# Two late turns of a local-attention loop put in the steady order, and the pool maxima of a later layer partly moved ahead and rebuffered

## The chip, the cores and the metric

The kernel runs on one core of one Trainium2 chip. The metric is device time of one launch in microseconds (us). The kernel before took 5015.74 us, the median of three runs (5015.45, 5015.74 and 5020.18). Five engines work beside each other: PE (TensorE, matrix products), DVE (VectorE), ACT (ScalarE), POOL (GpSimd) and SP (SyncE, which issues all DMA transfers, in one queue).

## The reference

The input is two images of 512 channels and 64 x 64 pixels, float32. Four residual layers follow one another, each `x = x + f(groupnorm(x))` with 32 groups:

- Layer 0, local and pooled attention with 8 heads of 64. Each pixel attends to its 3 x 3 neighbours and to 256 pooled tokens, with one softmax over both. A learned table adds to the nine local weights. The result goes through `W_proj`.
- Layer 1, deformable attention: offsets computed from the queries say where 256 keys are sampled from the image; then ordinary attention and an output product with `w_out`.
- Layer 2, a mixture of max pools. Seven pools with windows 1, 3, 5, 7, 9, 11 and 13 are made per channel, and a score of the channel mixes two neighbouring ones:

```
pools = jnp.stack([_maxpool_same(x, k) for k in KERNELS], axis=2)
...
return frac_b * b_out + frac_s * s_out + x
```

- Layer 3, linear attention with random exponential features (Favor), 256 features per head.

## The kernel before

Pixels are 4096 columns and channels are 4 chunks (KC) of 128 partitions. X holds the image and Y is a work area of the same size. A block is 512 columns (TB), one PSUM bank, and there are 8 blocks (NB). The two images are computed one after the other; `whole_net` calls layer0 to layer3 (L2748 to L2755) for each. All products are float32. A slower path (class General, up to L933) is compiled in behind a condition on the data and is not run here; what runs is class Net (from L934) with its helpers Queries and Local.

A tile framework schedules the program: by default it orders each engine's instructions by its own priorities. Inside `manual_schedule(engines={...})` the named engines run in the order in which the code issues. Buffers come from pools with a fixed number of copies, and a write waits until the last reader of the copy is done.

**Layer 0, class Local.** The work is cut into 16 units (4 chunks of channels by 4 strips of 1024 columns). `Local.run` (the loop at L2058) goes over turns i from -4 to 16. A turn interleaves stages of several units, one step of each in a round (`in_turn`, L51): norms and projections of unit i+3 (PE's L134), tap products of unit i+1 on DVE (`tap_products`, L2489: q times the shifted keys, into two product buffers `prods`), tap sums of unit i+1 on PE (`tap_sums`, L2527: into the one bank of the pool `l0t`; then DVE's L2536 multiplies, and ACT's L2538 takes the exponential out of that bank), softmax and values of unit i (`attend`, whose softmax sums are L2581 and L2584 and whose reciprocal chain on DVE is L2609 to L2612; L2616 and L2617 follow), and the weighting by the nine taps of unit i-1 (`weigh`, ACT L2656, DVE L2664, POOL L2669, which reads rows that SP fetches with L2640 and stores to a DRAM buffer `yd` with L2675).

`self.steady` (L2060) is true for turns 1 to 11. A steady turn runs PE in the written order, pairs the nine tap products as five DVE instructions of up to 1024 x 2 elements, spreads the steps of tap sums and projections over the rounds as a table says, and keeps the sums of two probabilities in two buffers of `sq`. Other turns run in the scheduler's order with nine single tap products. Turn 16 is in PE's written order as well. Unit 16 does not exist: turn 13 has no projections of queries and keys but the values of both of the last units, and turn 14 has the tap sums of the last unit. From turn 13 on `fetch_output` (L2231) loads W_proj into the four `sq` buffers, and turns 14, 15 and 16 begin the output products of the layer (`output`, L2242, L2258), which read `yd` back through SP (L2252).

**Layer 1.** After the attention blocks, `add_output` (L1215 on PE, L1218 and L1220 on DVE) writes the image back and takes its statistics. In the same loop DVE makes the first pool (window 3) for layer 2 in Y, by `maxima_across` and `maxima_down` (L1136 to L1152), through rows lent from the weights' buffer wkv. L1497 is the reciprocal of the softmax sums, which PE's L1505 spreads. The chain of small operations L1175 to L1207 (`pool_mixture`) works out the mixing weights, the last of which PE needs before layer 2 starts.

**Layer 2.** `pool_chunk` (L1363) runs per channel chunk. Steps j = 0 to 6 add the image and the six pools into eight PSUM banks, each as a product with a diagonal matrix: 8 blocks times two instructions of L1382 (ACT makes the diagonal, L1387). Each new pool from j = 2 is made on DVE from the last by a maximum of columns (`spread_max(h, last, 2)`) and one of rows; each is one operation of 128 x 3968 elements (L698), and ACT copies the two edges (L699). The pools pass through two buffers, and from chunk 1 on Y's last chunk is a third. From chunk 1, `maxima_below` (L1161 to L1166) first completes the rows of the first pool. Then ACT takes the sum out of the banks and, for chunks 0 to 2, its mean and variance come from sums (six small DVE operations per chunk, L1428 to L1436). In chunk 3 the eighth block's products of the first steps are held back, so that its bank serves for layer 3's group statistics (`stats_in_steps`: PE L965 and L970, DVE L966 to L972, POOL L973). Then DVE scales the first three parts of layer 3's two weight matrices by these (L978).

**Layer 3** begins with products of these scaled weights. SP loads its matrices Wk3 and Wv3 (L1359) and proj (L1521); L1522 is the first operation on proj.

Of the kernel before, what the change touches and what calls it, by code (L numbers as in the profile page):

```python
# [9 lines left out]
F32 = mybir.dt.float32  # L10
# [6 lines left out]
P = 128  # L17
# [916 lines left out]
class Net(General):  # L934
# [102 lines left out]
    def layer1(self, X, Y, d):  # L1037

        tc, nc, vec = self.tc, self.nc, self.vec
        with tc.tile_pool(name="l1", bufs=1) as sp:  # L1040
            wkv = sp.tile([P, KC, 2 * C], F32, name="wkv1")
# [4 lines left out]
            with tc.tile_pool(name="l1a", bufs=1) as wp, \  # L1046
# [6 lines left out]
            self.ahead = ExitStack()  # L1053
            dp = self.ahead.enter_context(tc.tile_pool(name="diags", bufs=1, side="right"))
            self.diags = cycle([dp.tile([P, P], F32, name=f"diag{i}") for i in range(2)])
            with tc.tile_pool(name="l1c", bufs=1) as late:

# [16 lines left out]
                with tc.tile_pool(name="l1b", bufs=2) as wp, \  # L1074
                        tc.tile_pool(name="l1s", bufs=6, space=PSUM) as pp, \
                        tc.tile_pool(name="l1o", bufs=2, space=PSUM) as ppo:
                    st = wp.tile([P, KC, NB, 6], F32, name="gn_st1", bufs=1)
                    w1 = wp.tile([P, KC, 32], F32, name="w1", bufs=1)
                    nc.sync.dma_start(w1, d["w1"].rearrange("(kc p) e -> p kc e", p=P))
                    w2 = wp.tile([32, C], F32, name="w2", bufs=1)  # L1080
                    nc.sync.dma_start(w2, d["w2"])
                    wo = wp.tile([P, KC, C], F32, name="wo1", bufs=1)
                    nc.sync.dma_start(wo, d["w_out1"].rearrange("(kc p) o -> p kc o", p=P))
                    steps = [(blk, cc) for blk in range(NB) for cc in range(KC)]
                    part = lambda blk, cc=slice(0, KC): Y[:, cc, blk * TB:(blk + 1) * TB]
                    flat = lambda a: a.rearrange("p k o -> p (k o)")
                    probs, totals, later = {}, {}, []
                    rows3 = flat(wkv)[:, :KC * 10 * W].rearrange("p (k y x) -> p k y x", k=KC, x=W)
                    ring = cycle([a[:, n:n + TB] for a, lo, hi in (
                        (flat(wq), 0, KC), (flat(wkv), 5, 8), (flat(feats), 0, 2),  # L1090
                        (wp.tile([P, 3 * TB], F32, name="totals", bufs=1), 0, 3))
                        for n in range(lo * TB, hi * TB, TB)]).__next__
                    for i in range(len(steps) + 4 + KC):
                        if i < len(steps):
                            blk, cc = steps[i]
                            probs[i], totals[i] = self.exponentials(part(blk, cc), keys[:, cc, :],
                                                                    ring, wp, pp)
                        if 1 <= i <= len(steps):
                            blk, cc = steps[i - 1]
                            self.attended(part(blk, cc), probs.pop(i - 1),  # L1100
                                          vals[:, :, cc * P:(cc + 1) * P], ppo)
                        at = lambda n: i >= n and (i - n) % KC == KC - 1 and (i - n) // KC
                        if (blk := at(1)) is not False and blk < NB:
                            r = self.inverse_sums([totals.pop(KC * blk + n) for n in range(KC)], wp,
                                                  pp)
                        if (blk := at(2)) is not False and blk < NB:
                            self.divided(part(blk), r, pp)
                        if (blk := at(3)) is not False and blk < NB:
                            later += [(blk, oc) for oc in range(KC)]
                        if later:  # L1110
                            blk, oc = later.pop(0)
                            self.add_output(X, wo, part(blk), blk, oc, st, pp)
                            if blk == NB - 1:
                                nc.vector.bn_aggr(self.mv[:, oc, :],
                                                  st[:, oc].rearrange("p b s -> p (b s)"))
                                if oc < 2:
                                    self.maxima_across(X, NB - 2, rows3, slice(oc, oc + 1))
                                    self.maxima_down(Y, NB - 2, rows3, slice(oc, oc + 1))
                            elif oc == KC - 1 and blk < NB - 2:
                                self.maxima_across(X, blk, rows3, slice(0, KC))  # L1120
                                self.maxima_down(Y, blk, rows3, slice(0, KC))
                    mixture = self.pool_mixture(w1, w2, wp, pp)
                    next(mixture)
                    self.maxima_across(X, NB - 1, rows3, slice(0, 1))
                    self.maxima_down(Y, NB - 1, rows3, slice(0, 1))
                    next(mixture)

    def maxima_across(self, X, blk, h, ks):
# [13 lines left out]
    def maxima_down(self, Y, blk, h, ks):  # L1142
# [7 lines left out]
        nc.vector.tensor_tensor(to, to, h[:, :, lo:rows + 1], ALU.max)  # L1150
        if blk == NB - 1:
            nc.vector.tensor_tensor(out[:, :, W - 1], h[:, :, rows], h[:, :, rows + 1], ALU.max)  # L1152

    def maxima_below(self, x, to, h, blk):

# [189 lines left out]

    def layer2(self, X, Y, d):

        self.w3 = self.ahead.enter_context(self.tc.tile_pool(name="l3w", bufs=2))
        self.wkv3 = [self.load3(d, name) for name in ("Wk3", "Wv3")]
        with self.tc.tile_pool(name="l2", bufs=1) as sp, \  # L1350
                self.tc.tile_pool(name="l2a", bufs=8, space=PSUM) as ppa:
            self.junk = sp.tile([P, TB], F32, name="pool_sq")
            self.accs = [ppa.tile([P, TB], F32, name=f"acc{b}", bufs=1) for b in range(NB)]
            for cc in range(KC):
                self.pool_chunk(X, Y, cc, self.mix[:, 7], self.mix[:, 8], self.mix[:, :7], sp)

    def load3(self, d, name):
        w = self.w3.tile([P, KC, C], F32, name="w3")
# [3 lines left out]
    def pool_chunk(self, X, Y, cc, c0, d0, wts, sp):  # L1362
# [2 lines left out]
        nc = self.nc  # L1365
        x2 = X[:, cc, :]
        image = lambda a: a.rearrange("p (y x) -> p y x", x=W)
        if cc == 0:
            self.scratch = sp.tile([P, N], F32, name="pool_h")
            self.pools = [sp.tile([P, N], F32, name=f"pool{i}") for i in range(2)]  # L1370
        else:
# [13 lines left out]
        def add(w, src, j):  # L1385
            dg = next(self.diags)
            nc.scalar.activation(dg, self.ident, AF.Copy, scale=w)  # L1387
            for b in range(NB):
# [3 lines left out]
                    product(b, dg, src, j)  # L1392
                while kept and j == 5 and b == 3:
                    product(*kept.pop(0))
            if len(kept) in (3, 5):
                next(stats, None)
            if len(kept) == 5:
                for w in self.wkv3:
                    self.scale_part(w, slice(0, KC - 1))

        add(c0[:, cc:cc + 1], x2, 0)
        flat = Y[:, cc, :]
        for j in range(1, 7):
            if j > 1:
                last, flat = image(flat), self.pools.pop(0)
                self.pools.append(flat)
                self.spread_max(h, last, 2)
                self.spread_max(image(flat), h, 1)
            add(wts[:, j, cc:cc + 1], flat, j)
        mv = self.mv[:, cc]  # L1410
        if cc == KC - 1:
# [8 lines left out]
        sums = sp.tile([P, 2, NB], F32, name="pool_sums", bufs=2)  # L1420
        shift = sp.tile([P, 1], F32, name="pool_shift", bufs=2)
# [10 lines left out]
        mean, var = mv[:, 0:1], mv[:, 1:2]  # L1432
        nc.vector.tensor_copy(mean, total[:, 0:1])
        nc.vector.tensor_tensor(shift, shift, mean, ALU.add)
        nc.vector.tensor_tensor(shift, shift, shift, ALU.mult)
        nc.vector.tensor_tensor(var, total[:, 1:2], shift, ALU.subtract)  # L1436

    def product_bound(self, q, keys, sp, pp):

# [528 lines left out]
class Local:  # L1968
# [78 lines left out]
    def run(self):  # L2047
# [311 lines left out]
    def projections(self, u, uvs, streams):  # L2359
# [506 lines left out]
```

## Time and profile before

The profile is one execution: it took 5015.88 us, of which the span from the first to the last instruction is 5014.0 us. PE's mean granted clock was 0.984 of full speed.

| what | value |
|---|---|
| median of three runs | 5015.74 us |
| the profiled execution | 5015.88 us |
| its span | 5014.0 us |
| DVE, ACT, POOL busy | 3074.1, 1816.8, 1859.1 us |
| a steady turn of layer 0 | 41.49 us |
| turns 12 and 13 of layer 0, image 1 | 45.90 and 50.32 us |
| layer 2, image 1 | 1486.9 to 1694 us |
| one operation L698 (128 x 3968) | 4.29 us |
| eight blocks of L1382 | 6.87 us |

The layers of image 1 lie at 31 to about 990 us (layer 0), to about 1487 (layer 1), to 1694 (layer 2) and to 2520 (layer 3); image 2 repeats them some 2489 us later. In the profile's rows an instruction is named by its line and its output and input tiles, and `xN` counts instructions in a group; a bracket at the end gives the idle time of the engine just before it and what ended that. A float32 product of one block is two PE instructions.

### The profile page before, as it was taken

What the parts mean: (1) busy time and instruction counts of PE and PEld (TensorE: products, weight loads), DVE (VectorE), ACT (ScalarE), POOL (GpSimd) and SP (SyncE); (2) the same over time, 40 slices, a digit from 0 to 9 for tenths busy, and PEclk for the clock granted to TensorE, in tenths of its full rate; (3) what the DMA queues carried; (4) which work ended last, traced back from release to release, by engine and by line L of the source; (5) the groups of instructions that cost most, each with busy time, mean ns of one, the idle gap of its engine ahead of it and who ended that gap; (6) DMA issues with size and microseconds to landing.
All of it is one profiled execution on the core that took longest, in us unless ns stands there. A gap on an engine that the chain in (4) does not pass through costs nothing. (4 is left out here: it accounts for less than half of the span.)

```text
span 5014.0 us, 48290 instructions
## 1 busy us (share of the span) xinstructions
PE 4771.4 (95%) x16883; PEld 1971.8 (39%) x16883; DVE 3074.1 (61%) x3958; ACT 1816.8 (36%) x3477; POOL 1859.1 (37%) x1220
## 2 busy tenths in 40 slices
PE   7999998999999999999999999989999999999998
PEld 3433332554334444433343333335543344444333
DVE  4367776744679533477732777767446794335776
ACT  1256664244323233322112566642443242333221
POOL 0046665501320145554500466654014101554554
PEclk9999999999999999999999999999999999999999
DMA  3035555500000000211120455555000000000111
GB/s 154 1 103 155 155 156 164 160 19 10 1 17 0 1 1 1 72 55 44 58 74 2 126 154 157 151 159 150 12 10 1 17 1 1 1 1 24 43 45 43
DMA packets 129440, 313.29 MB, mean 62 GB/s; under 512 B 23394, under 2 KB 36194, under 8 KB 127652
## 3 DMA queue, kind: packets, MB, share of 16 engines
q1 hardware_dynamic: 129188, 310.12, 21.6%
q8 instruction: 135, 2.21, 0.2%
q14 instruction: 117, 0.96, 0.1%
HBM read 260.73 MB, written 49.31 MB: 62 GB/s over the span
## 5 line engine op out<-in xcount | busy, mean ns | idle before, releaser
L134 PE MATMUL mm<-big,w 128*128 128x512 f32 x2496 | 1164.9, 610 | 16.3 <-DVE big L2448 11.5
L134 PEld LDWEIGHTS mm<-big,w 128*128 128x128 f32 x2496 | 452.6, 191 | 698.3 <-issue 557.2
L2669 POOL TENSOR_TENSOR late<-late,big 128x1024 f32<-128x1024 f32 x194 | 458.5, 2363 | 223.4 <-DVE big L2664 185.4
L2489 DVE TENSOR_TENSOR prods<-qs,big 128x1024 f32<-128x1024 f32 (+1 forms) x200 | 332.2, 1686 | 60.1 <-PE tap L2527 49.1
L1669 POOL TENSOR_TENSOR big<-big 128x512 f32<-128x512 f32 x224 | 277.8, 1273 | 219.4 <-ACT big L1660 219.4
L2664 DVE TENSOR_TENSOR big<-big,mm 128x512 f32<-128x512 f32 x388 | 253.1, 681 | 114.9 <-ACT mm L2656 107.0
L1660 ACT ACTIVATE big<-mm,ed 128x256 f32<-128x256 f32 x512 | 193.5, 489 | 233.1 <-DVE top L1656 200.7
L2656 ACT COPY mm<-big 128x512 f32<-128x512 f32 x432 | 245.8, 597 | 60.4 <-DMA big<-rows 25.1
L2574 POOL TENSOR_TENSOR late<-late 128x512 f32<-128x512 f32 x84 | 105.3, 1275 | 410.5 <-ACT late L2559 393.9
L2669 POOL TENSOR_TENSOR late<-late,tap 128x1024 f32<-128x1024 f32 x94 | 222.1, 2363 | 94.5 <-DVE tap L2664 80.1
L1472 POOL TENSOR_TENSOR wq<-prob 128x512 f32<-128x512 f32 x48 | 71.6, 1515 | 487.9 <-ACT prob L1469 476.5
L1656 DVE TENSOR_REDUCE top<-mm 128x1 f32<-128x512 f32 x256 | 159.0, 684 | 148.1 <-PE mm L1587 148.1
L1924 PE MATMUL mm<-k,w 128*128 128x512 f32 x512 | 235.1, 602 | 12.4 <-DVE k L1917 7.5
L134 PE MATMUL mm<-big,wq 128*128 128x512 f32 x512 | 236.7, 608 | 2.7 <-ACT off_t L1243 2.7
L1215 PE MATMUL mm<-big,wo 128*128 128x512 f32 x512 | 238.1, 611 | 0.0
L1382 PE MATMUL acc<-big,diag 128*128 128x512 f32 x512 | 228.7, 604 | 9.8 <-ACT diag L1387 4.6
L1634 PE MATMUL mm<-w,big 128*128 128x512 f32 x512 | 234.5, 601 | 0.0
L973 POOL TENSOR_TENSOR group_stats<-group_stats,cst 128x1 f32<-128x1 f32 (+1 forms) x20 | 20.2, 1025 | 566.4 <-DVE group_stats L972 510.2
L2527 PE MATMUL tap<-prods,cst 128*32 128x512 f32 x1152 | 189.6, 620 | 29.2 <-ACT late L2538 26.5
L1914 DVE RECIPROCAL psD<-psD 128x512 f32<-128x512 f32 x64 | 215.1, 3362 | 1.9
L134 PE MATMUL mm<-big,big 128*128 128x512 f32 x464 | 201.7, 594 | 0.5 <-DVE b_sr L1011 0.5
L1469 ACT ACTIVATE prob<-mm 128x512 f32<-128x512 f32 x256 | 133.2, 603 | 171.4 <-PE mm L1466 171.1
(428 smaller groups left out, 8114.1 us busy)
## 6 DMA issues: line engine op xcount, KB each, us to landing
big<-rows SPq DMA_DIRECT2D x432, 256.0 KB
tap<-rows SPq DMA_DIRECT2D x208, 256.0 KB
yd<-late SPq DMA_DIRECT2D x32, 512.0 KB
lost_all<-lost SPq DMA_DIRECT2D x128, 128.0 KB
out<-big SPq DMA_DIRECT2D x64, 256.0 KB
big<-in_W_kv SPq DMA_DIRECT2D x8, 1024.0 KB
rows<-late SPq DMA_DIRECT2D x64, 128.0 KB
big<-in_x SPq DMA_DIRECT2D x32, 256.0 KB
```

The lines of the kernel that those rows point to most:

```text
L134: self.nc.tensor.matmul(ps, w[:, kc, :], X[:, kc, blk * TB:(blk + 1) * TB], start=(kc == 0), stop=(kc == KC - 1))
L1215: nc.tensor.matmul(ps, w[:, kc, oc * P:(oc + 1) * P], att[:, kc, :], start=(kc == 0), stop=(kc == KC - 1))
L1382: nc.tensor.matmul(accs[b], dg, src[:, b * TB:(b + 1) * TB], start=(j == 0), stop=(j == 6))
L1634: nc.tensor.matmul(ps, X[:, kc, lo:lo + P], wv[:, kc, :], start=(kc == 0), stop=(kc == KC - 1))
L1660: nc.scalar.activation(f[:, t, :], pS[h][i][:, t % 2, :], AF.Exp, bias=ed[:, t, 2 * cc + h:2 * cc + h + 1])
L1669: nc.gpsimd.tensor_tensor(a, a, part, ALU.add)
L1914: nc.vector.reciprocal(psD, psD)
L1924: nc.tensor.matmul(ps, self.wo[:, kc, oc * P:(oc + 1) * P], qs[:, kc, :], start=(kc == 0), stop=(kc == KC - 1))
L2489: self.nc.vector.tensor_tensor(self.pair(u, k)[:, :n].rearrange("p k (y x) -> p k y x", x=W), bcast(qs.rearrange("p (y x) -> p y x", x=W), ...
L2656: nc.scalar.copy(ps, part)
L2664: nc.vector.tensor_tensor(part.rearrange("p (y x) -> p y x", x=W), self.vx[:, y:y + self.UY // 2, dx:dx + W], ps.rearrange("p (y x) -> p y ...
L2669: nc.gpsimd.tensor_tensor(out, out, t, ALU.add)
```

## The change

In layer 0, turns 12 and 13 count as steady (`units - 2` for `units - 4`), so they take PE's written order and all that hangs on `self.steady`. The table of the steps at which values are made gets two more entries, for the four values of turn 13.

```diff
-            self.steady = 1 <= i < units - 4
+            self.steady = 1 <= i < units - 2
...
-        made, taken = ((4, 6, 7, 8), (0, 2)) if self.steady else ((6, 7, 8, 9), (0, 3, 6, 9))
+        made, taken = ((4, 6, 7, 8), (0, 2, 4, 6)) if self.steady else ((6, 7, 8, 9), (0, 3, 6, 9))
```

In layer 1, the buffer wkv moves to a pool that lives until the end of layer 2 and serves there as the buffer h of column maxima (`self.scratch`). The first column maximum of chunk 0 (j = 2) is made in six pieces within layer 1's tail, and no longer in layer 2:

```diff
+        self.ahead, self.pooling = ExitStack(), ExitStack()
+        kept = self.pooling.enter_context(tc.tile_pool(name="kv1", bufs=1, side="right"))
+        wkv = kept.tile([P, KC, 2 * C], F32, name="wkv1")
+        self.scratch = wkv.rearrange("p k o -> p (k o)")
...
+                                for rows in ([(20, 32), (32, 44)], [(10, 20), (44, 55)],
+                                             [], [])[oc]:
+                                    self.across_rows(Y, slice(*rows))
...
                     self.maxima_down(Y, NB - 1, rows3, slice(0, 1))
+                    for rows in (0, 10), (55, W):
+                        self.across_rows(Y, slice(*rows))
                     next(mixture)
...
+    def across_rows(self, Y, rows):
+
+        image = lambda a: a.rearrange("p (y x) -> p y x", x=W)[:, rows]
+        self.spread_max(image(self.scratch), image(Y[:, 0, :]), 2)
```

In layer 2, chunk 0 has a third pool buffer, which is given up after it. Only then is the pool for layer 3's weights opened and Wk3 and Wv3 loaded. DVE runs chunk 3 in the written order. The statistics' steps stand in that order, the moments of chunks 0 to 2 are made at once in chunk 3, and ACT scales the weights in six copies:

```diff
+            with tc.tile_pool(name="l2f", bufs=1) as fp:
+                self.pools.append(fp.tile([P, N], F32, name="pool2"))
+                self.pool_chunk(X, Y, 0, c0, d0, wts, sp)
+                self.pools.pop(0)
+            self.w3 = self.ahead.enter_context(tc.tile_pool(name="l3w", bufs=2))
+            self.wkv3 = [self.load3(d, name) for name in ("Wk3", "Wv3")]
+            for cc in range(1, KC):
+                with (tc.manual_schedule(engines={mybir.EngineType.DVE}) if cc == KC - 1
+                      else nullcontext()):
+                    self.pool_chunk(X, Y, cc, c0, d0, wts, sp)
...
-            if len(kept) in (3, 5):
-                next(stats, None)
-            if len(kept) == 5:
-                for w in self.wkv3:
-                    self.scale_part(w, slice(0, KC - 1))
...
-                self.spread_max(h, last, 2)
+                if cc or j > 2:
+                    self.spread_max(h, last, 2)
                 self.spread_max(image(flat), h, 1)
+                if cc == KC - 1 and j in (4, 5):
+                    next(stats, None)
+                if cc == KC - 1 and j == 3:
+                    self.moments(sp)
+                if cc == KC - 1 and j == 5:
+                    for w in self.wkv3:
+                        for kc in range(KC - 1):
+                            nc.scalar.activation(w[:, kc], w[:, kc], AF.Copy,
+                                                 scale=self.stats[:, 1, kc:kc + 1])
...
-        total = sp.tile([P, 2], F32, name="pool_total", bufs=2)
-        nc.vector.tensor_reduce(total, sums, AX.X, ALU.add)
+
+    def moments(self, sp):
+
+        nc = self.nc
+        total = sp.tile([P, KC - 1, 2], F32, name="pool_total")
+        nc.vector.tensor_reduce(total, self.sums, AX.X, ALU.add)
```

The other five operations of `moments` are those of before, on three chunks' columns at once. The instructions' order on every engine outside these places is that of before.

More of the change, by code (lines that the diff above doesn't have):

```diff
@@ L1039, in layer1 @@
         tc, nc, vec = self.tc, self.nc, self.vec
+        self.ahead, self.pooling = ExitStack(), ExitStack()
+        kept = self.pooling.enter_context(tc.tile_pool(name="kv1", bufs=1, side="right"))
+        wkv = kept.tile([P, KC, 2 * C], F32, name="wkv1")
+        self.scratch = wkv.rearrange("p k o -> p (k o)")
         with tc.tile_pool(name="l1", bufs=1) as sp:
-            wkv = sp.tile([P, KC, 2 * C], F32, name="wkv1")
             nc.sync.dma_start(wkv, d["w_kv1"].rearrange("(kc p) o -> p kc o", p=P))
@@ L1052, in layer1 @@
                 self.query_and_sample(X, Y, wq, bq, grid, feats, top, wp, pp, ppk)
-            self.ahead = ExitStack()
-            dp = self.ahead.enter_context(tc.tile_pool(name="diags", bufs=1, side="right"))
+            dp = self.pooling.enter_context(tc.tile_pool(name="diags", bufs=1, side="right"))
             self.diags = cycle([dp.tile([P, P], F32, name=f"diag{i}") for i in range(2)])
@@ L1087, in layer1 @@
                     probs, totals, later = {}, {}, []
-                    rows3 = flat(wkv)[:, :KC * 10 * W].rearrange("p (k y x) -> p k y x", k=KC, x=W)
+                    rows3 = self.scratch[:, :KC * 10 * W].rearrange("p (k y x) -> p k y x", k=KC, x=W)
                     ring = cycle([a[:, n:n + TB] for a, lo, hi in (
@@ L1346, in layer2 @@
     def layer2(self, X, Y, d):
[L1348 to L1351, printed above, removed]
+        tc = self.tc
+        with tc.tile_pool(name="l2", bufs=1, side="right") as sp, \
+                tc.tile_pool(name="l2a", bufs=8, space=PSUM) as ppa:
             self.junk = sp.tile([P, TB], F32, name="pool_sq")
             self.accs = [ppa.tile([P, TB], F32, name=f"acc{b}", bufs=1) for b in range(NB)]
-            for cc in range(KC):
-                self.pool_chunk(X, Y, cc, self.mix[:, 7], self.mix[:, 8], self.mix[:, :7], sp)
+            self.sums = sp.tile([P, KC - 1, 2, NB], F32, name="pool_sums")
+            self.shifts = sp.tile([P, KC - 1], F32, name="pool_shift")
+            self.pools = [sp.tile([P, N], F32, name=f"pool{i}") for i in range(2)]
+            c0, d0, wts = self.mix[:, 7], self.mix[:, 8], self.mix[:, :7]
+            with tc.tile_pool(name="l2f", bufs=1) as fp:
[8 more added lines that the diff above has]
+                    self.pool_chunk(X, Y, cc, c0, d0, wts, sp)
+        self.pooling.close()
     def load3(self, d, name):
@@ L1367, in pool_chunk @@
         image = lambda a: a.rearrange("p (y x) -> p y x", x=W)
[L1368 to L1371, printed above, removed]
+        if cc:
             self.maxima_below(x2, Y[:, cc, :], self.scratch, NB - 1 if cc == 1 else NB - 2)
@@ L1419, in pool_chunk @@
             return
-        sums = sp.tile([P, 2, NB], F32, name="pool_sums", bufs=2)
-        shift = sp.tile([P, 1], F32, name="pool_shift", bufs=2)
+        sums, shift = self.sums[:, cc], self.shifts[:, cc:cc + 1]
         blocks = [x2[:, b * TB:(b + 1) * TB] for b in range(NB)]
@@ L1428, in pool_chunk @@
             nc.scalar.activation(self.junk, xx, AF.Square, bias=shift, accum_out=sums[:, 1, b:b + 1])
-        total = sp.tile([P, 2], F32, name="pool_total", bufs=2)
-        nc.vector.tensor_reduce(total, sums, AX.X, ALU.add)
+    def moments(self, sp):
+        nc = self.nc
+        total = sp.tile([P, KC - 1, 2], F32, name="pool_total")
+        nc.vector.tensor_reduce(total, self.sums, AX.X, ALU.add)
         nc.vector.tensor_scalar(total, total, 1.0 / N, None, ALU.mult)
[L1432 to L1436, printed above, removed]
+        mean, var = (self.mv[:, :KC - 1, i] for i in range(2))
+        nc.vector.tensor_copy(mean, total[:, :, 0])
+        nc.vector.tensor_tensor(self.shifts, self.shifts, mean, ALU.add)
+        nc.vector.tensor_tensor(self.shifts, self.shifts, self.shifts, ALU.mult)
+        nc.vector.tensor_tensor(var, total[:, :, 1], self.shifts, ALU.subtract)
     def product_bound(self, q, keys, sp, pp):
```

## The prediction

> **What bounds the kernel now.** I read the busy shares first, then PE's waits, then a table by stretches, then the timelines of the stretches that the change touches.
>
> ```profile
> span 5014.0 us, 48290 instructions
> ...
> PE 4771.4 (95%) x16883; PEld 1971.8 (39%) x16883; DVE 3074.1 (61%) x3958; ACT 1816.8 (36%) x3477; POOL 1859.1 (37%) x1220
> ```
>
> PE bounds the whole: it is idle for 5014.0 - 4771.4 = 242.6 us, and no edit here takes a product from it. A gain can only be PE idle time, or time at its half clock behind an idle stretch. PE's list of waits says whose idle time it is:
>
> ```profile
> PE tap L2527 <- ACT late L2538: 26.5, 6, 8.3
> ...
> PE acc L1382 <- DVE pool L698: 6.4, 4, 1.6
> ...
> PE acc L1382 <- DVE group_stats L972: 4.9, 2, 2.4
> ```
>
> The first is the tap sums of layer 0 (26.5 us in 6 waits), the others are layer 2. Stretches of image 1, cut at the end of the softmax sums (L2584) of turns 11, 12 and 13, with a steady turn ahead of them and chunks 0 to 3 of layer 2 behind:
>
> ```profile
> 692.38:733.87 41.49, 40.79 (x149) 12.87 (x149) 32.50 (x49) 25.46 (x46) 26.26 (x14) 1.00 0.60 156
> 743.24:789.14 45.90, 45.09 (x162) 14.02 (x160) 34.82 (x55) 26.67 (x47) 28.57 (x15) 1.00 0.52 145
> 789.14:839.46 50.32, 46.00 (x151) 14.58 (x149) 32.25 (x53) 24.98 (x44) 26.05 (x14) 0.93 0.57 157
> ...
> 1533.00:1583.00 50.00, 48.34 (x113) 21.26 (x113) 46.44 (x22) 17.87 (x52) 0.00 (x0) 1.00 0.00 0
> ```
>
> Columns: length, busy time of PE, weight load, DVE, ACT, POOL, then granted clock. A steady turn takes 41.49 us and PE is busy for 40.79 of it; turns 12 and 13 take 45.90 and 50.32, the latter at clock 0.93. The two waits are in PE's timeline:
>
> ```profile
> 798.07 1.92 PE L2527 MATMUL tap<-prods,cst 128*32 128x512 f32 x2 [4.23 <-ACT late L2538]
> 799.91 8.74 PE L134 MATMUL mm<-big,w 128*128 128x512 f32 x16
> ...
> 848.75 5.33 PE L2527 MATMUL tap<-prods,cst 128*32 128x512 f32 x18 [8.23 <-ACT late L2538]
> ```
>
> The tap sums have one PSUM bank. Unit n+1's first matmul waits until ACT's exponential (L2538) has read unit n's, and that waits for L2536 on DVE, which ends at about 848.1 behind products and transposes. In layer 2 the bound is DVE, 4.29 us an operation, with two holes in chunk 0 and 1 and a slower chunk 3:
>
> ```profile
> 1510.95 4.29 DVE L698 TENSOR_TENSOR pool<-pool_h 128x3968 f32<-128x3968 f32 x1 [2.19 <-PE acc L1382]
> ...
> 1543.31 4.29 DVE L698 TENSOR_TENSOR big<-pool_h 128x3968 f32<-128x3968 f32 x1 [2.80 <-ACT pool_h L699]
> ...
> 1678.95 2.46 DVE L978 TENSOR_SCALAR w<-w,group_stats 128x512 f32<-128x512 f32 x6 [0.75 <-POOL group_stats L973]
> ```
>
> [...] behind the 4.23 us wait, 16 instructions of L134 take 8.74 us against 7.26 elsewhere, and there are half-clock windows of 6.8 us (from 796.3) and 10.2 us (from 844.1). [...] the edge copy L699 sits behind ACT's evacuations of chunk 0. [...] Here L1136 took 1.72 us at 1447.16, with POOL's L1472 running, and 0.66 at 1451.87.
>
> **Layer 0, turns 12 and 13.** Putting PE in the written order makes both turns like the eleven before; PE's order of the changed kernel repeats the steady cycle there. If they keep 41.49 us, turn 12's sums end at 743.24 + 41.49 = 784.73 (before 789.14, 4.4 gained) and turn 13's at 826.22 (before 839.46, 13.2 gained). As a check, PE's busy time at full clock in these turns: 45.09 + 46.00 less half of 10.2 + 6.8 us, and less some 5 us because tap matmuls issued in nine pieces do not pair (36 instructions 7.7 us, against 5.0), is about 78, within 2 × 41.49 = 83. DVE is busy 32.50 of 41.49 in a steady turn, so it has room.
>
> Turn 14 stays in the scheduler's order, so it inherits the hazard: taps of unit 14 -> L2536 -> L2538 -> taps of unit 15. In DVE's order of the changed kernel only the reciprocal chain (about 1.4 us) and one product stand ahead of L2536, where before four products and the 2.37 us L2616 did; I put PE's wait at 1.5 to 2 us instead of 8.23. Then PE is paced by nine single products of some 1.14 us. The last taps end at about 846.4, against 862.2 before: 15.8 gained. Since that second part rests on an order only, I take **14 us per image** (8 to 17).
>
> Moved past on SP: the three later W_proj loads into the squares' buffers now come together behind turn 13's sums, and the second fetch of yd stands behind four tap fetches. By issue times in the trace it would land near 850, and is needed near 853: nothing, with 3 us of cover. The output products behind them shift as a block, PE 95% busy.
>
> **Layers 1 and 2.** The pool maximum of chunk 0's first step (4.29 us) is cut into six pieces in layer 1's tail. [...] Two pieces of 12 rows stand in DVE's queue ahead of the last reciprocal L1497. DVE has no gap from 1433 to 1456 and PE already waits 1.14 us for that reciprocal, so 1.9 us goes straight to PE. The middle two fit DVE's idle 1.95 at 1466.6. The last two stand around the last statistics, where DVE was idle for 0.41: +1.1. So PE begins layer 2 at 1487.38 + 3.0 = 1490.4, DVE's first 4.29 us operation at 1489.9 instead of 1486.88.
>
> DVE removed: 4.29 and the 2.19 us buffer wait in chunk 0 (third pool buffer), the moments' six small operations in chunks 0 to 2 (mostly hidden, 0.15 us each), and 2.46 + 0.75 of scaling in chunk 3, which goes to ACT (6 × 0.6 = 3.6 us, ACT is busy 20.6 of 61 there). Added: L1522 behind the proj load, 0.5; one block of moments in chunk 3, 6 × 0.15 = 0.9; two waits for PE's statistics now in line with DVE's order, 0.4 each. Queued behind such a wait are all later maxima. The edge-copy hole of 2.80 stays at about 2.2. The chunks on DVE: chunk 0 is nine operations of 4.40 and 0.5, ending at 1489.9 + 40.1 = 1530.0 (before 1532.88); chunk 1 is ten of 4.40, 3.2 for the rows below (L1161 to L1166) and the hole of 2.2, so 1579.4 (1582.92); chunk 2 takes its present 49.93, so 1629.3 (1632.85); chunk 3 takes its present 52.76 less 3.2 plus 0.9 + 0.8 and some 0.4 of hand-over, so about 1680.9 (1685.61).
>
> PE alone needs 7 × 6.867 = 48.07 per chunk, so from 1490.4 it would end chunk 3 at 1490.4 + 192.3 + 2.7 (half clock) = 1685.4 with no wait. It must wait for DVE in chunk 3: its products of the fifth step start when DVE gives that pool, two operations before its last, near 1671.8, and 18.0 us of products remain (21 of 0.858: two steps of eight, and the five of the last block kept back), so 1689.8, or up to 1691.6 with a half-clock window. Before: 1693.6. Gain **3.5 us per image** (-3 to +8: -3 is PE's late start with no DVE gain kept, +8 is PE without waits, 1693.6 - 1685.4). Unknown here: the proj load is now issued at about 1487, takes 2 us and more, and DVE's second operation would wait for it if late (0 to 2 us, taken 0); POOL blocking the pieces (0 to 1.1 us each, for the first two, taken 0). Wk3/Wv3 loads go from 1476.6 to about 1527, needed near 1672: hidden by 145 us.
>
> **Sum.** Per image 14 + 3.5 = 17.5; two images 35. From the profiled run's own time, 5015.88 (span 5014.0, with 1.9 around it): 5015.9 - 35 = **4981 us**. The median of the three runs is 5015.74, so nothing changes.
>
> **Rivals.** 0.2%, 10 us, is about what a measurement of this kernel can tell from no change.
>
> A, PE-bound layer 2: DVE keeps ahead in chunk 3. For it: PE has 3 to 4 us of waiting left in my sum. Against: the in-line waits. (16 + 8) × 2 = 48 gives 4968.
>
> B, layer 2 gives nothing: POOL stretches the pieces, the statistics waits cost more. For: 1.72 against 0.66. 28 us: 4988; with -3 per image, 4994.
>
> C, turn 13 does not keep pace, since its row fetches or products come late: only turn 12's 4.4 stays. For: DMA share 0.60. Against: eleven turns alike. (4.4 + 3.5) × 2 = 16: 5000.
>
> D, slower: SP is one queue; W_proj loads wait there for the buffers that turn 13's sums now read, and every row fetch of turn 14 and the yd store stand behind them. Each us of waiting beyond slack passes by L2664 and POOL to the output products. It must cost over 17.5 + 5 = 22.5 us per image to end above 5026; a turn's transfers are 0.60 × 41.5 = 25 us, so only a full turn's fetches held back does it: 17.5 - 25 = -7.5 per image, 5031. Against: before, SP's fetches pause from 842 to 850 there at no visible cost.
>
> **Chances.** Forecast (4974 to 4986) 0.48; A 0.17; B 0.16; C 0.12 (of it 0.06 within 0.2%); D 0.07. Range 4963 to 5002: it leaves out about a third of A's low side, half of C and D. Faster by over 0.2%: 0.87; within: 0.06; slower: 0.07.
>
> **What would show it.** Right: the L2538 wait falls from 26.5 to about 6 us in all; L2584 marks 41.5 us apart through turn 13; no 10 us half-clock window at 844; no 2.19 wait in chunk 0, no L978 in chunk 3 on DVE, chunk ends some 3 us earlier and PE's first layer-2 product 3 us later. Wrong: the 8.2 us wait reappearing in turn 13 or 14; new waits of PE for DMA after turn 13; L1497 more than 2 us later; long waits of DVE for PE's statistics in chunk 3.

## The result, and the profile after

The changed kernel took 4987.23 us, the median of four runs (4983.79 to 4990.30), against 5015.59 us for the kernel before in the same comparison: 28.4 us less, ratio 0.9941 with a 95% interval of 0.9924 to 0.9958. The forecast was 4981 us, 35 less, with a range of 4963 to 5002. The profiled execution took 4990.09 us, the second slowest of the four; its span is 4988.3, which is 25.7 less than the span before. In what follows a half-clock window is a stretch in which the profile's clock record grants PE half its speed (0.50; in the changed kernel, for one, from 852.2 to 859.0).

The page's first lines, in the manner of before:

```profile
span 4988.3 us, 48282 instructions
...
PE 4760.9 (95%) x16883; PEld 1970.3 (39%) x16883; DVE 3069.9 (62%) x3916; ACT 1825.6 (37%) x3499; POOL 1861.7 (37%) x1220
```

PE executes the same 16883 products. Its idle time is 4988.3 - 4760.9 = 227.4 us, 15.2 less than before, and its busy time is 10.5 us less. At half speed some 6.6 us of that is time that went with the windows: PE was busy for 125.8 us of half-clock windows before and for 112.5 now. The rest was not followed up. PE's list of waits in the changed kernel (lines from 1043 on are numbered up to 29 higher than before: L2527, L2538, L2565, L2661 are now L2556, L2567, L2594, L2690, and L2258 is L2287):

```profile
PE mm L2594 <- DVE late L2690: 12.9, 4, 5.0
...
PE tap L2556 <- DVE prods L2518: 7.4, 16, 1.3
...
PE mm L1187 <- DVE channels_mv L1116: 5.7, 2, 2.8
PE acc L1403 <- DVE group_stats L972: 5.4, 2, 2.7
...
PE mm L1534 <- DVE recip L1526: 4.3, 2, 2.1
...
PE tap L2556 <- ACT late L2567: 3.5, 2, 1.8
```

The wait of the tap sums is 3.5 us in two pieces where it was 26.5 in six. The wait of layer 2 for DVE's pools (6.4) is off the list, the one for L972 stays. Two lines are new in size: the first, 3.0 us before (2 times, 1.5 the longest) and 12.9 now, and the sums' wait for DVE's products, 2.7 before and 7.4 now.

Stretches of image 1 again, cut at the end of the sums of turns 11, 12, 13 and 14 (columns as before: length, busy PE, weight load, DVE, ACT, POOL, clock):

```profile
744.34:785.83 41.49, 40.79 (x150) 12.87 (x148) 32.47 (x48) 25.52 (x45) 26.27 (x14) 1.00 0.55 150
785.83:827.32 41.49, 40.79 (x150) 12.87 (x148) 32.62 (x48) 25.25 (x44) 26.34 (x15) 1.00 0.64 182
827.32:884.80 57.48, 47.17 (x151) 19.04 (x149) 37.74 (x49) 19.35 (x35) 34.47 (x17) 0.94 0.64 182
```

Turns 12 and 13 are steady turns to a hundredth. Turn 14 takes 57.5 us, where before it took 52.4 (839.46 to 891.90), but it also has 12 more of PE's instructions in it (151 for 139), so these two lengths can't be compared as they are. From the end of the last taps to the end of turn 14's sums PE runs the same 79 instructions in both kernels: this takes 29.64 us before in both images, and 36.22 and 35.82 us now. So part of the gain is given back at once, in the first turn that is not in the written order.

The whole by stages, from the two traces (first instruction of the sums to the last output product; from there to the second matmul of the mixture; to layer 2's first product; to its last; the rest up to the next image's sums or the end), in us. The last output product of layer 0 ends at 1015.5 us before, later than the 990 given for the layer above, since the first products of layer 1's norm run between the last ones:

| stage | image 1 before, after | gain | image 2 before, after | gain |
|---|---|---|---|---|
| layer 0 from turn 0's sums | 729.85, 720.11 | 9.74 | 728.71, 718.72 | 9.99 |
| layer 1 up to the mixture | 464.64, 468.32 | -3.68 | 464.65, 468.31 | -3.66 |
| to layer 2's first product | 7.23, 7.23 | 0 | 7.22, 7.22 | 0 |
| layer 2 | 206.38, 198.53 | 7.85 | 206.38, 198.56 | 7.82 |
| layer 3 and what follows | 1081.35, 1085.20 | -3.85 | 831.95, 829.27 | 2.68 |

With 1.1 us lost ahead of the first sums these give the 25.7 us between the spans. Layer 3 was not touched. Between these two executions its change has different signs in the two images, and in the other profiled runs below it ranges from 1084.7 to 1090.6 and from 829.2 to 832.7. Half-clock windows lie at other places there in each run: in image 1 they add up to 27.3 us before and 37.6 after, in image 2 to 26.1 and 19.7. At half speed these differences are worth up to 5.1 us lost and 3.2 gained, which is about what the table has. It is counted as scatter.

### The profile page after: what moved, and what is told of

Read it like the earlier page. It is cut to its first block, busy times and chain, and to the rows that moved or that the text cites. A ratio compares the mean times of both kernels' runs of the same rounds, so it can differ in the third digit from the quotient of the medians.

```text
span 4988.3 us, 48282 instructions
## 1 busy us (share of the span) xinstructions
PE 4760.9 (95%) x16883; PEld 1970.3 (39%) x16883; DVE 3069.9 (62%) x3916; ACT 1825.6 (37%) x3499; POOL 1861.7 (37%) x1220
## 5 line engine op out<-in xcount | busy, mean ns | idle before, releaser
L134 PE MATMUL mm<-big,w 128*128 128x512 f32 x2496 | 1162.1, 608 | 19.1 <-DVE big L2477 13.6
L2518 DVE TENSOR_TENSOR prods<-qs,big 128x2048 f32<-128x2048 f32 (+1 forms) x184 | 330.7, 1819 | 34.8 <-PE tap L2556 24.2
L2685 ACT COPY mm<-big 128x512 f32<-128x512 f32 x432 | 245.3, 597 | 82.7 <-DMA big<-rows 49.8
L1501 POOL TENSOR_TENSOR wq<-prob 128x512 f32<-128x512 f32 x48 | 71.9, 1519 | 491.3 <-ACT prob L1498 479.8
L2556 PE MATMUL tap<-prods,cst 128*32 128x512 f32 x1152 | 183.2, 604 | 11.5 <-DVE prods L2518 7.4
```

The lines of the kernel that those rows point to most:

```text
L134: self.nc.tensor.matmul(ps, w[:, kc, :], X[:, kc, blk * TB:(blk + 1) * TB], start=(kc == 0), stop=(kc == KC - 1))
L2518: self.nc.vector.tensor_tensor(self.pair(u, k)[:, :n].rearrange("p k (y x) -> p k y x", x=W), bcast(qs.rearrange("p (y x) -> p y x", x=W), ...
L2685: nc.scalar.copy(ps, part)
```

## Experiments: which part gives what

**Layer 0 alone**: the kernel before with the two edited lines of layer 0.

```diff
-            self.steady = 1 <= i < units - 4
+            self.steady = 1 <= i < units - 2
...
-        made, taken = ((4, 6, 7, 8), (0, 2)) if self.steady else ((6, 7, 8, 9), (0, 3, 6, 9))
+        made, taken = ((4, 6, 7, 8), (0, 2, 4, 6)) if self.steady else ((6, 7, 8, 9), (0, 3, 6, 9))
```

> The kernel before with only the two edited lines of layer 0 (turns 12 and 13 steady, four value steps). Theory: the parts do not touch each other, and layer 0 gives what the two traces show between the first softmax sums and the last output product, 9.7 us in image 1 and 10.0 in image 2, so about 20 us less than before: 4996 us. Rival, the forecast's own 14 us per image, hidden in the whole change by something that layer 2 takes back: 28 less, 4988. PE's 4.8 us wait at L2594/L2565 in turn 14 should be there as in the whole change.

Measured: 4995.33 us, ratio 0.9965 (0.9951 to 0.9978). Layer 0 takes 720.10 and 717.67 us, and PE waits 4.77 us for L2661 in turn 14 at 854.91. The theory of 20 us holds, and the interval leaves out the rival's 28. Which part of what hangs on `self.steady` gives the gain (PE's written order, the paired products or the two buffers of `sq`) was not taken apart.

**The pools alone**: the changed kernel with those two lines put back.

> The changed kernel with turns 12 and 13 put back (units - 4, two value steps), so only the layer 1 and 2 part. Theory: about 4.2 us per image as between the two traces (3.7 lost ahead of layer 2, 7.85 gained in it): 8.4 less than before, 5007 us. Rival: in-line waits take it back, no difference from 5015.7.

Measured: 5007.36 us, ratio 0.9981 (0.9974 to 0.9988), some 9.5 us less than before. Layer 1's end takes 466.37 us in both images, 1.7 more than before, so of the 3.7 us in the changed kernel about 2 are a half-clock window that this run does not have (3.4 us, at 1190.1 there). Layer 2 takes 199.8 us in both images, 6.6 less than before. In it PE has 8.7 us of half clock before, 7.2 in this run and 4.6 in the changed kernel, so about 2 us of the 7.85 in the table are half-clock time as well. The two parts add, within the intervals: 9.5 us here and 21.6 in the run with layer 0 alone, against 28.4.

## Experiments: turn 14

DVE's L2690, for which PE waits in turn 14, waits itself for ACT's copies L2685, and these for fetched rows. SP's issues in the changed kernel (start, duration, line, transfer):

```profile
835.12 1.10 SPq L2651 DMA_DIRECT2D rows<-late  x2
836.32 0.54 SPq L2281 DMA_DIRECT2D big<-yd  x1
846.70 0.33 SPq L2704 DMA_DIRECT2D yd<-late  x1
847.20 1.12 SPq L2669 DMA_DIRECT2D big<-rows  x2
848.42 1.18 SPq L2669 DMA_DIRECT2D tap<-rows  x2
```

and ACT and PE behind them:

```profile
852.44 1.11 ACT L2685 COPY mm<-big 128x512 f32<-128x512 f32 x2 [8.56 <-DMA big<-rows]
```

```profile
854.40 3.93 PE L2594 MATMUL mm<-late,vp 128*64 128x512 f32 x8 [4.78 <-DVE late L2690]
```

The store of unit 12 into yd stands ahead of turn 14's row fetches and waits until POOL has made its last sum (a row of POOL ends at 846.67). SP stands still for 9.8 us, though the rows' own stores were issued at 835.12. In the kernel before, the same store was issued behind the first four fetches:

```profile
850.54 1.11 SPq L2640 DMA_DIRECT2D big<-rows  x2
853.09 1.09 SPq L2640 DMA_DIRECT2D tap<-rows  x2
856.80 0.33 SPq L2675 DMA_DIRECT2D yd<-late  x1
```

**The store behind the fetches**: the scheduler is told to put it behind the first six fetches, nothing else.

```diff
             self.fetch_tap(u, i)
+        if self.unstored:
+            with self.net.tc.issue_after(self.fetched):
+                self.unstored.pop()()
...
-        nc.sync.dma_start(self.yd[:, cc, lo:lo + self.UT], out)
+        store = lambda: nc.sync.dma_start(self.yd[:, cc, lo:lo + self.UT], out)
+        if u == KC * self.UN - 4:
+            self.unstored.append(store)
+        else:
+            store()
```

> The changed kernel, with unit 12's yd store put behind the first six row fetches of turn 14 in SP's queue, nothing else moved. Theory: in turn 14 the store waits on SP for POOL's last add (ends 846.7) and holds the row fetches behind it, ACT's copies wait 8.6 us for them, DVE's L2690 5.6 and PE 4.8, then a half-clock window of 6.8 us. With the fetches ahead, they are issued near 838 and PE's wait falls below 1 us: 4 to 7 us less per image, about 4976 us. Rival: the rows come late in any case (their own store lands late, or the second yd fetch now lands late), the wait stays or moves to the output products: 4987 us, no difference.

Measured: 4977.75 us, ratio 0.9921 (0.9908 to 0.9935) against 0.9941 for the changed kernel. SP in this kernel:

```profile
833.78 1.10 SPq L2652 DMA_DIRECT2D rows<-late  x2
834.98 1.09 SPq L2282 DMA_DIRECT2D big<-yd  x2
839.46 1.11 SPq L2670 DMA_DIRECT2D big<-rows  x2
842.91 1.08 SPq L2670 DMA_DIRECT2D tap<-rows  x2
845.35 1.08 SPq L2670 DMA_DIRECT2D big<-rows  x2
846.48 0.58 SPq L2709 DMA_DIRECT2D yd<-late  x1
```

The first rows are fetched 7.7 us earlier (6.4 if counted from the stores of rows ahead of them, which are 1.3 earlier too), and the second fetch of yd, which the changed kernel issued at 854.71, has moved up with them. L2595 (the L2594 of the changed kernel) starts at 848.21 with no wait, and in image 1 the half-clock windows at 852.2 (6.8 us) and 968.2 (3.4 us) are gone. The 79 instructions behind the last taps take 30.56 us in both images, 5.7 and 5.3 less than in the changed kernel. Layer 0 takes 712.80 and 715.06 us, 7.3 and 3.7 less. Both differ from 5.7 and 5.3 by 1.6, about what one window of 3.4 us takes at half speed: in image 1 that at 968.2 is gone, in image 2 one came later in the layer. The rival, rows that are late in any case, falls.

## Experiments: layers 1 and 2

**No pieces ahead**: the first column maximum of chunk 0 is one operation at layer 2's start, held there behind the mixing weights.

```diff
-                                for rows in ([(20, 32), (32, 44)], [(10, 20), (44, 55)],
-                                             [], [])[oc]:
-                                    self.across_rows(Y, slice(*rows))
...
-                    for rows in (0, 10), (55, W):
-                        self.across_rows(Y, slice(*rows))
...
-                if cc or j > 2:
+                with (self.tc.issue_after(self.mixed) if not cc and j == 2 else nullcontext()):
                     self.spread_max(h, last, 2)
```

> The changed kernel with no pieces ahead: the first column maximum of chunk 0 is one operation of 4.29 us again, at the start of layer 2 behind the mixing weights. Theory: layer 1's tail gets back its 464.65 us between the last output product of layer 0 and the statistics of the mixture (468.3 in the changed kernel), and layer 2 grows by the 4.29 us that DVE has more ahead of chunk 3's fifth step (198.5 to some 202.8). The pieces as placed are worth only 0.6 us per image: about 4988.5 us, not to be told from 4987.2. Rival: PE hides most of the 4.29 in layer 2, and the kernel without pieces is faster by up to 3.7 us per image: 4980. Second rival: the pieces are worth their whole 4.29, and it is slower by 8: 4995.

Measured: 4995.82 us, ratio 0.9957 (0.9943 to 0.9970). This interval overlaps the changed kernel's (0.9924 to 0.9958), so the traces have to decide. My theory falls and the second rival's size is right, but not by its reason. Layer 1's end is 464.56 us as expected. Layer 2 is 206.06, not 202.8. PE's timeline shows why. In the changed kernel only two waits of PE are there behind layer 2's first product:

```profile
1653.68 6.25 PE L1403 MATMUL acc<-big,diag 128*128 128x512 f32 x14 [0.34 <-DVE group_stats L966]
...
1662.74 3.67 PE L1403 MATMUL acc<-pool,diag 128*128 128x512 f32 x8 [2.69 <-DVE group_stats L972]
```

In this run there are four:

```profile
1570.17 7.11 PE L1398 MATMUL acc<-pool,diag 128*128 128x512 f32 x16 [1.67 <-DVE pool L698]
...
1620.16 25.13 PE L1398 MATMUL acc<-big,diag 128*128 128x512 f32 x58 [1.68 <-DVE big L698]
...
1653.42 6.25 PE L1398 MATMUL acc<-big,diag 128*128 128x512 f32 x14 [2.01 <-DVE group_stats L966]
...
1662.48 5.37 PE L1398 MATMUL acc<-pool,diag 128*128 128x512 f32 x8 [2.69 <-DVE group_stats L972]
```

PE waits 1.67 + 1.68 + 2.01 + 2.69 = 8.05 us against 3.03, and has a half-clock window of 3.4 us at 1662.5 besides. Counted from layer 2's first product, the fifth step of chunk 3 starts at 186.1 us against 180.3: 5.8 later, and the window adds 1.7. I had let DVE's lateness grow by 4.29 only: two waits of DVE for the edge copies (0.66 and 0.54), which its lead hides in the changed kernel, come back too. So the pieces, even badly placed, are worth 7.5 - 3.8 = 3.7 us per image in these traces; of the 3.8 about 2 are the window at 1190.1.

**Two buffers**: no third pool buffer in chunk 0.

```diff
-            with tc.tile_pool(name="l2f", bufs=1) as fp:
-                self.pools.append(fp.tile([P, N], F32, name="pool2"))
-                self.pool_chunk(X, Y, 0, c0, d0, wts, sp)
-                self.pools.pop(0)
+            self.pool_chunk(X, Y, 0, c0, d0, wts, sp)
```

> The changed kernel without the third pool buffer in chunk 0. Theory: DVE waits about 2.2 us in chunk 0 for PE to free a buffer, all later maxima come that much later, and PE's wait ahead of chunk 3's fifth step grows from 2.7 to 4.9 us: layer 2 from 198.5 to 200.7, and 4.4 us more in all, about 4991.6. Rival: PE is ahead of DVE only by luck and the wait is hidden, no difference: 4987.

Measured: 5005.87 us, ratio 0.9975 (0.9965 to 0.9985): some 17 us slower than the changed kernel, not 4.4. DVE's timeline:

```profile
1496.03 4.29 DVE L698 TENSOR_TENSOR wkv<-pool 128x3968 f32<-128x3968 f32 x1
1506.62 4.29 DVE L698 TENSOR_TENSOR pool<-wkv 128x3968 f32<-128x3968 f32 x1 [6.30 <-PE acc L1400]
```

The wait is 6.30 us and not 2.19. It ends when PE gives up a buffer, 23.3 us after PE's first product of layer 2 (23.6 in the kernel before), whenever DVE arrives; DVE now arrives one operation (4.29) earlier and waits about that much longer. Layer 2 takes 205.91 us, as without the pieces (206.06) and as before the change (206.38). One of the two alone gives layer 2 next to nothing; both together bring it to 198.5. Both of these runs have chunk 3's written order and the joined moments, which were not tried singly.

**Scaling on DVE**: the six scalings of layer 3's weights, in DVE's written order again.

```diff
-                        for kc in range(KC - 1):
-                            nc.scalar.activation(w[:, kc], w[:, kc], AF.Copy,
-                                                 scale=self.stats[:, 1, kc:kc + 1])
+                        self.scale_part(w, slice(0, KC - 1))
```

> The changed kernel with the six scalings of layer 3's weights on DVE again, in its written order behind the statistics' last step (6 operations, 2.46 us, and a wait of up to 0.75 for POOL). Theory: DVE's last pool is ready at 1671.3 in the changed kernel and PE takes it at 1673.97, so 2.7 us of the 3.2 are hidden: layer 2 grows by 0.5 us, about 4988.2. Rival, the sum in the forecast, which took DVE as the bound to the end of chunk 3: 3.2 us per image, 4993.6.

Measured: 4991.48 us, ratio 0.9948 (0.9934 to 0.9961), within the scatter of the changed kernel's 0.9941. The trace decides:

```profile
1655.32 2.47 DVE L978 TENSOR_SCALAR w<-w,group_stats 128x512 f32<-128x512 f32 x6 [0.97 <-POOL group_stats L973]
```

DVE loses 0.97 + 2.47 = 3.4 us, and PE waits 0.71 for the last pool in image 1 and not at all in image 2. Layer 2 is 199.14 and 199.76 us, 0.6 and 1.2 more; the 1.2 of image 2 is half-clock time (7.1 us in layer 2 there, 4.7 in the changed kernel). The rival's 3.2 us per image does not appear.

**Pieces in the gaps**: the pieces at other places in DVE's queue; two behind the products by the reciprocal (`self.quotient`), two behind the statistics of output chunks, and the last two in the idle time of the mixing weights' chain (`self.shifted_mean` is L1209's instruction).

```diff
-                                for rows in ([(20, 32), (32, 44)], [(10, 20), (44, 55)],
-                                             [], [])[oc]:
-                                    self.across_rows(Y, slice(*rows))
+                                for rows, held in (
+                                        [((20, 32), self.quotient), ((32, 44), self.quotient),
+                                         ((44, 55), last.ins)], [((10, 20), last.ins)], [], [])[oc]:
+                                    with tc.issue_after(held):
+                                        self.across_rows(Y, slice(*rows))
...
-                    for rows in (0, 10), (55, W):
-                        self.across_rows(Y, slice(*rows))
+                    with tc.issue_after(last.ins):
+                        self.across_rows(Y, slice(0, 10))
                     next(mixture)
+                    with tc.issue_after(self.shifted_mean):
+                        self.across_rows(Y, slice(55, W))
```

> The changed kernel, with the six pieces of the first column maximum moved in DVE's queue: the two of 12 rows from ahead of the last reciprocal to behind the products by it (a hole of 1.9 us), 11 and 10 rows behind the statistics of output chunks 0 and 1, 10 and 9 rows into DVE's idle time within the chain of mixing weights. Theory: the pieces in the path cost what layer 2's start lost, 3.7 us per image (1.0 at the reciprocal, 0.9 at the last statistics, the rest by the clock); nearly all comes back, layer 2 begins 2 to 3.5 us earlier, and the time falls by 4 to 7 us to about 4982. Rival: the loss is from elsewhere (clock windows, POOL), no difference. Second rival: DVE in chunk 3 then bounds, and the gain at the start is lost at the fifth step.

Measured: 4974.26 us, ratio 0.9918 (0.9905 to 0.9932). PE in the changed kernel:

```profile
1450.77 1.14 PE L1534 MATMUL mm<-recip,cst 2*128 2x512 f32 x8 [2.12 <-DVE recip L1526]
1451.84 19.13 PE L1227 MATMUL mm<-big,wo 128*128 128x512 f32 x40
```

and in this run:

```profile
1444.43 1.14 PE L1539 MATMUL mm<-recip,cst 2*128 2x512 f32 x8
1445.51 17.43 PE L1232 MATMUL mm<-big,wo 128*128 128x512 f32 x40
1464.92 0.39 PE L1191 MATMUL mm<-channels_mv,cst 128*128 128x4 f32 x2 [1.98 <-DVE channels_mv L1116]
```

The wait for the reciprocal is gone (2.12 in the changed kernel, 1.14 before), and with it the half-clock window behind it: the 40 instructions of L1232 take 17.43 us against 19.13. The wait for the statistics is 1.98 as before the change. Layer 1's end takes 461.8 us, 6.5 less than in the changed kernel, more than my 3.5. The two waits are 3.0 of it. The rest is half-clock time, 12.1 us in this stretch of the changed kernel and 3.4 here; among it is the window at 1190.1, far ahead of the pieces, which their place doesn't explain. Layer 2 keeps its 198.7.

**Both moves** together.

> Both moves together: the yd store behind the row fetches, and the six pieces in DVE's gaps. Theory: they lie in different layers and add, 9.5 and 13 us below the changed kernel in the medians: about 4965 us. Rival: part of each gain was the phase of the clock's windows, which together may not repeat: 4970 to 4974.

Measured: 4967.29 us, ratio 0.9899 (0.9884 to 0.9914), faster than both kernels. The two moves add: they take 0.0020 and 0.0023 off the changed kernel's ratio singly and 0.0042 together. The median speaks against the rival's 4970 to 4974, but the interval, some 4960 to 4975 us, does not leave it out. The page:

```profile
span 4968.4 us, 48284 instructions
...
PE 4754.6 (96%) x16883; PEld 1967.0 (40%) x16883; DVE 3068.0 (62%) x3916; ACT 1823.2 (37%) x3499; POOL 1862.4 (37%) x1220
```

## Why the forecast was right, and where it was off

The direction, the order of size and all mechanisms but one were right; the forecast took 6.6 us too much off. Some of the nearness is luck: in the profiled execution about 2 us per image of layer 1's loss and about 2 of layer 2's gain are half-clock time that the forecast did not have, and they cancel.

- **Turns 12 and 13**: forecast 41.49 us each and 13.2 us gained at turn 13's sums. Measured 41.49 and 41.49; the sums begin 539.5 us after turn 0's, before 552.8: 13.3. The forecast's sum of PE's busy time in these turns has a slip: it takes off half of the 10.2 us window from 844.1, which lies behind turn 13's end at 839.46. Without it the sum is 91.1 - 3.4 - 5 = 82.7 us, just within 83 instead of 5 below; PE was busy for 2 × 40.79 = 81.6.
- **Turn 14's first taps**: forecast a wait of 1.5 to 2 us, then a pace set by single products on DVE. Measured 1.77 (PE's L2556 at 835.51), then two of 1.27 for products; the last taps end 14.8 us earlier by the same count, forecast 15.8.
- **What failed: "Moved past on SP", which was taken at nothing.** I counted the W_proj loads and the second yd fetch, and left out the yd store, which had moved ahead of the row fetches in the same queue. It put 4.8 us of waiting, with a half-clock window of 6.8 us at its end, into the first image, 5.0 and 3.4 into the second, and of the 14.8 us at the last taps 9.7 were left at the end of the layer (10.0 in the second image). With the store behind the fetches the gain over before is 17.1 and 13.7, on average 15.4, half-clock windows included: the forecast of the turn itself was good. The second fetch of yd was not issued near 850 either, but at 854.71. Rival D had the right queue and mechanism, with the W_proj loads in the store's place; its price there was far below the 22.5 us at which it would have decided.
- **Layer 1's end**: forecast 3.0 later. Measured 3.7, of it 1.0 at the reciprocal (1.9 forecast) and 0.9 at the statistics (1.1). The rest is the window at 1190.1; the run with the pools alone shows 1.7. The forecast's 1.9 is two pieces of 12 rows (744 elements), of which a line through two traced operations of before, 4.29 us for 3968 elements and 0.80 for 620 (L1161 at 1532.99), makes 0.93 each (0.80 and 0.74 for the last two, of 10 and 9 rows). Traced, five of the six pieces took 0.73 to 0.92 us, and the second of 12 rows 2.00. It runs from 1442.08, and L1143 just ahead of it took 1.14 us against 0.66 at 1445.98; POOL's L1501 ran from 1440.28 to 1443.3. Before, L1136 and L1138 took 1.72 and 1.57 us at 1447.16 and 1448.99, with POOL's L1472 running from 1447.08 to 1450.0, against 0.66 and 0.69 just after. Beside POOL two DVE operations were thus 1.9 us longer in all before and two 1.6 now, which is part of the difference. That POOL is the cause was not tested, and the rest was not followed up.
- **Layer 2**: forecast 199.4 to 201.2 us from its first to its last product, measured 198.5. The wait ahead of the fifth step in chunk 3, forecast as what decides, is there: 2.69 us, put down to L972, which follows the fifth pool on DVE and ends 0.1 us after it. DVE's chunks end within 2 us of where the sum put them, counted from PE's start. Net of the late start: 4.2 per image, forecast 3.5.
- Some terms of that sum do not stand alone. The 2.19 us buffer wait and the 4.29 of the moved operation are one thing: with the pieces ahead and two buffers DVE waits 6.30, nearly all of the 6.48 that the sum took off for both. And the 3.2 us of scaling are nearly all slack, since PE's last step starts 2.7 us after DVE's last pool is ready.

## What to carry to other kernels

When a stage's order changes, go through every instruction of each in-order queue that it shares and ask what the new head waits for: here a store that waited for a late result held every fetch behind it on SP for 9.8 us, though the transfers have nothing to do with each other. The wait for a pool buffer was set by the engine that frees it: it ended 23.6 us after PE's first product of layer 2 in the kernel before and 23.3 after it with two buffers, and DVE, one operation of 4.29 us earlier there, waited 6.30 us and not 2.19. So work moved ahead and the buffer that lets it run ahead must be priced together. Small operations moved into a busy engine cost little in its idle stretches: with the six pieces there, PE's wait for the last reciprocal was gone and that for the statistics was 1.98 us, as before the change. Ahead of what the bound engine waited for they lengthened its wait (here by 1.0 and 0.9 us), and a half-clock window can come on top (3.4 us from 1452.9 behind the longer wait for the reciprocal).

## What was not expected of the hardware

The trace of before has windows of 6.8 and 10.2 us at PE's waits of 4.23 and 8.23 us. That the short waits in layer 1 bring none, as I had priced them, was not shown there. In these runs windows also lie behind waits of 1.13 to 2.13 us, but not always. PE's wait ahead of the products of the last reciprocal can be followed through all ten traces, in two images each. In the two runs with the pieces in the gaps it is gone: no half-clock window lies behind it in any of the four cases, and the 40 instructions of the output product take 17.43 us. Where it is 1.13 or 1.14 us, five of six cases have a window of 3.4 us (in the kernel before from 1458.5) and one has none. Where it is 2.11 to 2.13 us, seven of ten have a window of 3.4 us (in the changed kernel from 1452.9), one has 6.8 us, and two have none. The 40 instructions take 18.8 to 19.1 us with a window of 3.4, 20.3 with 6.8, and 17.43 with none. So these waits of PE came with about 1.7 us more than their own length, or 3, or nothing. In the traces of before and of the changed kernel all half-clock windows, 28 and 25, start on one grid of 3.41 us, which lies differently in the two. Whether a wait's place on this grid decides was not tested. One stage can differ by 5 us within a single trace: in the run with two buffers, layer 1's end takes 468.29 us in one image and 463.03 in the other.
